# A selective-scan kernel: C rows held in SBUF between groups, their products written into b's buffers, the middle group's partitions in two halves

## The chip, the cores and the metric

One core of one Trainium2 chip runs the whole program. The metric is device time in microseconds of one execution, the median of three runs. All arithmetic that matters here is float32.

## The reference

Two "metaformer" layers on an image batch x of shape (2, 96, 128, 128). Layer 0 adds a four-direction Mamba block to the channel-normalised image, then a small quantised MLP; layer 1 adds a 3x3 convolution and another MLP. The Mamba block is what the change touches, and it takes most of the time. For each of four directions (rows, rows reversed, columns, columns reversed) and each position t of the 16,384 positions, with 192 inner channels d and 16 states s:

```
xc, z  = split(x @ in_w.T);  xc = silu(causal_conv4(xc) + conv_b)
dt_raw, B, C = split(xc @ xproj_w.T)          # 6, 16 and 16 numbers a position
dt = softplus(dt_raw @ dt_w.T + dt_b);  A = -exp(A_log)
h[d,s] = exp(dt[d] * A[d,s]) * h[d,s] + dt[d] * xc[d] * B[s]
y[d]   = sum_s h[d,s] * C[s] + Dp[d] * xc[d]
out    = (y * silu(z)) @ outp_w.T             # four directions joined by fuse_w
```

B and C depend on the position and the state, not on the channel. Each direction has its own.

## The kernel before

Each image of the batch goes through three stages: a normalisation, the Mamba stage (`mamba`), and the MLPs with the convolution (`ffn_and_conv`). Only the Mamba stage changes.

**Tiling.** Two directions are handled together (`PAIRS`): 2 x 192 = 384 channels are three groups (g = 0, 1, 2) of 128 partitions. Group 0 holds channels of the first direction, group 2 of the second, and group 1, the middle one, 64 of each. A step is 512 positions of one pair of directions: 32 steps for each of two pairs, so 64 for an image and 128 in all. Within a step and a group the 16 states are taken two at a time; such a pair of states is a unit, eight to a group (numbered 0 to 7 here) and 24 to a step. Four states, two units, are a quad.

**A unit's work.**

- ACT computes the decay exp(dt * A) into a PSUM tile `da`, two activations of 512 (`decay`, L349).
- DVE scans along the positions, once for each state (`scan`, L353). The result h replaces `da` in PSUM, or, for units in `BY_POOL`, the b tile in SBUF.
- h is multiplied by the C rows (128x1024): by DVE (L441) into the tile that holds the C rows, or by POOL in place for units in `BY_POOL` (L360), which here are units 0 and 4 of each group.
- PE adds the two halves of the product into one PSUM tile y by matmuls with the identity (`sums`, L357). An fp32 matmul shows as two PE instructions.
- Once in a quad, POOL multiplies the B rows (128x2048) by dt * xc in place (`b_part`, L339), two units ahead of the scan, and adds the entry state.

At a group's start DVE multiplies the finished y by silu(z) (`gated`, L364), and y's only buffer starts afresh with a matmul pair (L448). In the first and third group of a step PE also projects a finished group (`project`, L372 and L374).

**B and C rows.** They are computed as 64 rows of 512 numbers and stored in DRAM (`rows_to_dram`, L277). For each quad, two transfers bring the B rows (`row0`) and the C rows (`row1`) back, each spread over 128 partitions, 1 MB (`row_tile`, L335): 24 in a step. B has four buffers, fetched three quads ahead; C three, fetched two quads ahead. In the middle group the two directions lie on alternate partitions, so that one transfer serves both. To bring xc and silu(z) of the middle group into that order, ACT writes them to a tile `mix`, and two transfers of 64 partitions each put them on alternate partitions (`mix`, L256). The weights of the middle group are permuted to match (`_layout`, `perm`).

**Order.** It is written out by hand. Iteration k issues the first scan of unit k, then the product, the end-state copy (L442) and the sums of unit k-1 (`behind`), then the decay of unit k+2 and the second scan of unit k. Work of the next step (convolutions, gates, rows, dt) has fixed places in this order. `later(k, where, ...)` puts a job at iteration k, after its first part (0) or at its end (1): POOL's product of a `BY_POOL` unit at the end of the iteration after the unit, its sums two iterations later. All of the row transfers are issued by SP, in order; a transfer whose buffer is not yet free holds up those behind it. Which buffer a new tile takes is settled when the program is built: the one that comes free first in the written order.

Of the kernel before, what the change touches and what calls it, by code (L numbers as in the profile page):

```python
# [10 lines left out]
F32 = mybir.dt.float32  # L11
# [3 lines left out]
AF = mybir.ActivationFunctionType  # L15
ALU = mybir.AluOpType
# [13 lines left out]
HID = 384  # L30
PAIRS = ((0, 2), (1, 3))
NG = 3
B_AHEAD = 3
C_AHEAD = 2
AHEAD = 2
BY_POOL = tuple((g, s) for g in range(3) for s in (0, 8))
BCO = 32
NBC = 4 * S

# [2 lines left out]
def tile_metaformer(ctx: ExitStack, tc: tile.TileContext, a: dict, out: bass.AP):  # L42
# [142 lines left out]
    def mamba(acc, xnr, xnc):  # L185

        with ExitStack() as st:
            pool = lambda n, bufs, **kw: st.enter_context(tc.tile_pool(name=n, bufs=bufs, **kw))

            io, gen, one, mixp, two = (pool(*p) for p in (("io", 2), ("gen", 4), ("one", 1), ("mixp", 1), ("two", 2)))  # L190
            ps_w, ps_y, ps_m = (pool(n, k, space=PSUM) for n, k in (("ps_w", 3), ("ps_y", 1), ("ps_m", 1)))
            rows_d = pool("rows_d", 3, space=DRAM)

# [20 lines left out]
            def prologue(pi, i, d):  # L214
# [20 lines left out]
                def conv_out(g):  # L235
                    if g == 1:
                        d["xc"] = two.tile([128, NG, T], F32, name="xc")
                    t = mixed("xc") if g == 1 else d["xc"][:, g, :]
                    nc.scalar.activation(t, d["ps"], AF.Identity, bias=convb[:, pi, g : g + 1])  # L239

                def gate(g):
                    d["ps"] = inproj(pi, g, lambda dd, k, lo, hi: inz[:, dd, lo:hi], src, (3,))
# [1 line left out]
                def gate_out(g):  # L244
                    if g == 1:
                        d["sz"] = two.tile([128, NG, T], F32, name="sz")
                    nc.scalar.copy(mixed("sz") if g == 1 else d["sz"][:, g, :], d["ps"])  # L247

                def mixed(name):
                    d["mix", name] = mixp.tile([128, T], F32, name="mix")  # L250
                    return d["mix", name]

                def mix(name):

                    for k in range(2):
                        nc.sync.dma_start(d[name][k:128:2, 1, :], d["mix", name][64 * k : 64 * k + 64, :])  # L256

                def silu(name):
                    nc.scalar.activation(d[name], d[name], AF.Silu)
# [45 lines left out]


                first = pi == 0 and i == 0
                at = [(-3, 1, load), (3, 0, partial(mix, "xc")), (11, 0, partial(silu, "xc"))]
                at += [(9, 0, partial(mix, "sz")), (31, 1, partial(silu, "sz"))]
                at += [(12, 0, rows), (13, 1, rows_out), (14, 0, rows_to_dram)]  # L310
                for g, k in ((1, 1), (0, 5), (2, 9)):
                    at += [(k, 0, partial(conv, g)), (k + 1, 1, partial(conv_out, g))]
# [13 lines left out]
                at = [(k, where, getattr(f, "func", f) not in outs, f) for k, where, f in at]  # L326
                return sorted(at, key=lambda p: p[:3])

            def row_tile(d, g, s, k, ahead):

                t = gen.tile([128, 4, T], F32, name=f"row{k}", bufs=ahead + 1)

                src = d["bcd"][k, s // 4] if g == 1 else d["bcd"][k, s // 4, g // 2 : g // 2 + 1]
                n = src.shape[0]
                nc.sync.dma_start(t, src[None].broadcast_to((128 // n, n, 4, T)))  # L335
                return t

            def b_part(i, d, g, s, b):
                nc.gpsimd.tensor_tensor(b, d["dtu"][g][:, None, :].broadcast_to((128, 4, T)), b, ALU.mult)  # L339
# [17 lines left out]
                    nc.tensor.matmul(y, ident, c[:, j, :], start=False, stop=s + j == S - 1)  # L357

            def by_pool(h, c):
                nc.gpsimd.tensor_tensor(c, h, c, ALU.mult)  # L360

            def gated(pi, d, g, y):
                t = d["sz"][:, g, :]
# [26 lines left out]
            def later(k, where, rank, f, *args):  # L390
                todo.setdefault((k, where), []).append((rank, partial(f, *args)))
# [20 lines left out]
            prepare(1)  # L412
            bs, cs, das, hs, quads = {}, {}, {}, {}, {}

            def fetch(k, n, ahead, m):
                if k < total:
                    t = row_tile(state[k // nu], *units[k % nu], n, ahead)
                    m[k], m[k + 1] = t[:, 0:2, :], t[:, 2:4, :]
                    if n == 0:
                        quads[k] = t  # L420

            def feed(k):

# [11 lines left out]
            def behind(k):  # L435

                n, u = divmod(k, nu)
                (pi, i), d, (g, s) = steps[n], state[n], units[u]
                h, c = hs.pop(k), cs.pop(k)
                if (g, s) not in BY_POOL:  # L440
                    nc.vector.tensor_tensor(c, h, c, ALU.mult)  # L441
                nc.scalar.copy(hst[:, g, s : s + 2], h[:, :, T - 1])  # L442
                if s == 0:
                    if k > 0:
                        pn, pu = divmod(k - 1, nu)
                        gated(steps[pn][0], state[pn], units[pu][0], ys.pop(k - 1))
                    y = ps_y.tile([128, T], F32, name="y")
                    nc.tensor.matmul(y, dmat[:, pi, g, :], d["xc"][:, g, :], start=True, stop=False)  # L448
                else:
                    y = ys.pop(k - 1)  # L450
                ys[k] = y
                if (g, s) in BY_POOL:
                    later(k + 1, 1, True, by_pool, h, c)
                    later(k + 3, 1, True, sums, s, y, c)
                else:
                    sums(s, y, c)
                if k == total - 1:
                    gated(pi, d, g, y)
                if s == S - 2 and g > 0:
                    later(k + 4, 0, True, project, pi, i, d, g)  # L460
                    later(k + 5, 1, False, collect, pi, d, g)

            for m, (n, ahead) in ((bs, (0, B_AHEAD)), (cs, (1, C_AHEAD))):
                for k in range(ahead):
                    fetch(2 * k, n, ahead, m)
            feed(0)
            for k in range(AHEAD):
                feed_decay(k)
            for k in range(total + 6):
                n, u = divmod(k, nu)  # L470
                if u == nu - 3:

                    prepare(n + 2)
                if k % 2 == 0:
                    fetch(k + 2 * B_AHEAD, 0, B_AHEAD, bs)
                    feed(k + AHEAD)
                issue(k, 0)
                if k < total:
                    (g, s) = units[u]
                    da, b = das.pop(k), bs.pop(k)  # L480
                    hs[k] = b if (g, s) in BY_POOL else da
                    scan(0, da, b, hs[k])
                if 0 < k <= total:
                    behind(k - 1)
                feed_decay(k + AHEAD)
                if k < total:
                    scan(1, da, b, hs[k])
                if k % 2 == 0:
                    fetch(k + 2 * C_AHEAD, 1, C_AHEAD, cs)
                issue(k, 1)  # L490

    def ffn_and_conv(b, acc):
# [107 lines left out]
def _layout(v):  # L600

    f = np.float32
    order = [d for pair in PAIRS for d in pair]

    perm = np.arange(2 * DI)
    perm[128:256] = perm[128:256].reshape(2, 64).T.reshape(-1)
    grouped = lambda w: w.reshape(2, NG, 128, -1).transpose(2, 0, 1, 3)
    plain = lambda w: grouped(w[order].reshape(2, 2 * DI, -1))
    rows = lambda w: grouped(w[order].reshape(2, 2 * DI, -1)[:, perm])
    xw = v["L0_conv_xproj_w"]  # L610
    bcw = np.zeros((2, 2 * DI, BCO + NBC), f)
    dtw = np.zeros((2 * RK, 2, 2 * DI), f)
    for pi, pair in enumerate(PAIRS):
        for k, d in enumerate(pair):
            at = slice(k * DI, (k + 1) * DI)
            for j in range(2):

                to = [BCO + 2 * j * S + 8 * (s // 4) + 4 * k + s % 4 for s in range(S)]
                bcw[pi, at, to] = xw[d, RK + j * S : RK + (j + 1) * S]
            bcw[pi, at, k * RK : (k + 1) * RK] = xw[d, :RK].T  # L620
            dtw[k * RK : (k + 1) * RK, pi, at] = v["L0_conv_dt_w"][d].T
    outx = np.zeros((C, 2, NG + 1, 128), f)
    for pi, (p, q) in enumerate(PAIRS):
        ow = v["L0_conv_outp_w"]
        outx[:, pi, 0] = ow[p, :, :128]
        outx[:, pi, 1, 0::2] = ow[p, :, 128:]
        outx[:, pi, 2, 1::2] = ow[q, :, :64]
        outx[:, pi, 3] = ow[q, :, 64:]
    out = {
        "x": v["x"].reshape(NB, C, L),  # L630
        "ident": np.eye(128, dtype=f),
        "inx": v["L0_conv_in_w"][:, :DI].transpose(2, 0, 1),
        "inz": v["L0_conv_in_w"][:, DI:].transpose(2, 0, 1),
        "taps": v["L0_conv_conv_w"].transpose(0, 2, 1)[None],
        "convb": plain(v["L0_conv_conv_b"])[..., 0],
        "bcw": grouped(bcw[:, perm]),
        "dtw": dtw[:, :, perm],
        "dtb": rows(v["L0_conv_dt_b"])[..., 0],
        "alog": rows(v["L0_conv_A_log"]),
        "dskip": rows(v["L0_conv_Dp"])[..., 0],  # L640
        "outx": outx,
        "fusew": v["L0_conv_fuse_w"].reshape(C, 4, C).transpose(2, 1, 0),
        "fuseb": v["L0_conv_fuse_b"].reshape(C, 1),
        "kw": v["L1_conv_kernel"].transpose(1, 2, 3, 0).reshape(C, 9, C),
    }
    for n in range(2):
        p = f"L{n}_ffn_"
        out[f"w1_{n}"] = v[p + "W1"].T
        out[f"b1_{n}"] = v[p + "b1"].reshape(3, 128).T
        out[f"w2_{n}"] = v[p + "W2"].T.reshape(3, 128, C).transpose(1, 0, 2)  # L650
        out[f"b2_{n}"] = v[p + "b2"].reshape(C, 1)
    return {k: np.ascontiguousarray(w) for k, w in out.items()}
# [16 lines left out]
```

## Time and profile before

| | us |
|---|---|
| median of 3 runs | 11546.39 (11545.31 to 11548.33) |
| the profiled execution, its own time | 11556.77 |
| its span | 11555.0 |
| DVE busy | 10421.6 |
| PE busy | 10435.0 |
| POOL busy | 9672.3 |
| ACT busy | 7901.7 |
| POOL b products (L339), 1536 | 6948.9, mean 4.524 |
| DVE scans (L353), 4608 into da and 1536 into row | 5456.9 and 1852.4, means 1.214 and 1.206 |
| DVE C products (L441), 2304 | 2776.7, mean 1.205 |
| POOL C products (L360), 768 | 1807.4, mean 2.353 |
| DVE gated products (L364) | 264.6, mean 0.689, idle ahead of them 229.5 |
| row transfers, 3072 of 1 MB | median 7.4 from issue to landing |

3416.96 MB were moved by DMA. A group's line on the page gives its busy time, its mean in ns, and the idle time of the engine just before its instructions with what ended it. A wait line gives the waiting engine and line, what it waited for, the total in us, the times and the longest. A timeline line gives start, duration, engine, line, operation and tiles; "x3" stands for three merged in a row. DVE instructions overlap slightly: one starts about 1.12 us after the one before, though each record is 1.2 long.

### The profile page before, as it was taken

How to read it: one execution, taken by the hardware profiler on the slowest of the kernel's cores; microseconds unless marked ns; L12 is line 12 of the kernel's file. 1: busy time of each engine (PE TensorE's matmuls, PEld its weight loads, DVE VectorE, ACT ScalarE, POOL GpSimd, SP SyncE). 2: the span in 40 equal slices, each digit the busy share in tenths (PEclk: the TensorE clock that was granted, in tenths of full speed). 3: DMA queues.
4: the chain of work that ended last, by engine and by line, in shares of the span. 5: the costliest groups of instructions: out<-in, count | busy, mean ns of one | idle time of the engine just before them, and what ended most of it. 6: DMA issues, size and time to landing. Idle time of an engine off the chain costs nothing. (4 is left out here: it accounts for less than half of the span.)

```text
span 11555.0 us, 94102 instructions
## 1 busy us (share of the span) xinstructions
PE 10435.0 (90%) x24208; PEld 3971.4 (34%) x24208; DVE 10421.6 (90%) x10127; ACT 7901.7 (68%) x13564; POOL 9672.3 (84%) x4700
## 2 busy tenths in 40 slices
PE   7999999999999999989989999999999999999899
PEld 2333333333333333333323333333333333333333
DVE  6999999999999999994469999999999999999944
ACT  6767767677677677665567677677676776776655
POOL 5999999999999999991159999999999999999911
PEclk8999999999999999999989999999999999999999
DMA  7888888888888888880068888888888888888800
GB/s 263 335 329 333 333 332 332 330 331 333 329 332 333 330 331 333 329 322 19 26 243 334 328 331 334 330 333 333 333 331 329 332 332 329 331 333 329 319 13 13
DMA packets 540755, 3416.96 MB, mean 296 GB/s; under 512 B 67532, under 2 KB 68652, under 8 KB 143832
## 3 DMA queue, kind: packets, MB, share of 16 engines
q1 hardware_dynamic: 539960, 3410.16, 76.8%
q8 instruction: 196, 3.21, 0.1%
q14 instruction: 343, 2.81, 0.1%
q0 software_dynamic: 256, 0.79, 0.0%
HBM read 3289.04 MB, written 54.53 MB: 289 GB/s over the span
## 5 line engine op out<-in xcount | busy, mean ns | idle before, releaser
L339 POOL TENSOR_TENSOR row<-dtu,row 128x2048 f32<-128x2048 f32 x1536 | 6948.9, 4524 | 283.3 <-DMA row<-bcd 281.6
L357 PE MATMUL y<-row,ident 128*128 128x512 f32 x12288 | 5690.6, 603 | 700.0 <-DVE row L441 699.9
L353 DVE TENSOR_TENSOR_SCAN da<-da,row 128x512 f32<-128x512 f32 x4608 | 5456.9, 1214 | 38.9 <-ACT da L349 5.2
L349 ACT ACTIVATE da<-dt,amat 128x512 f32<-128x512 f32 x6144 | 4246.9, 691 | 170.2
L357 PEld LDWEIGHTS y<-row,ident 128*128 128x128 f32 x12288 | 2256.8, 190 | 4008.4 <-issue 2243.5
L441 DVE TENSOR_TENSOR row<-da,row 128x1024 f32<-128x1024 f32 x2304 | 2776.7, 1205 | 70.2 <-DMA row<-bcd 70.0
L442 ACT COPY hst<-da 128x2 f32<-128x2 f32 x2304 | 368.9, 160 | 2652.2 <-DVE row L441 2649.3
L360 POOL TENSOR_TENSOR row<-row,row 128x1024 f32<-128x1024 f32 x768 | 1807.4, 2353 | 223.0 <-DVE row L353 147.5
L353 DVE TENSOR_TENSOR_SCAN row<-da,row 128x512 f32<-128x512 f32 x1536 | 1852.4, 1206 | 91.9 <-POOL row L339 84.1
L211 PE MATMUL misc<-xa,inx 96*64 96x512 f32 (+1 forms) x2048 | 946.1, 605 | 50.0 <-ACT mix L239 26.8
L211 PE MATMUL misc<-xb,inx 96*64 96x512 f32 (+1 forms) x2048 | 952.3, 608 | 33.6 <-ACT hst L442 24.2
L564 POOL TENSOR_TENSOR acc<-acc,y 96x512 f32<-96x512 f32 x128 | 147.4, 1151 | 991.5 <-DVE y L563 991.5
L298 POOL TENSOR_TENSOR dtu<-dt,xc 128x512 f32<-128x512 f32 x384 | 487.4, 1269 | 106.0 <-DMA xb<-xnc 99.8
L576 PE MATMUL pc<-pad,kw 96*96 96x512 f32 x1152 | 566.4, 593 | 0.0
L211 PEld LDWEIGHTS misc<-xa,inx 96*64 96x64 f32 (+1 forms) x2048 | 327.3, 165 | 581.2 <-issue 438.0
L448 PE MATMUL y<-xc,dmat 128*128 128x512 f32 x768 | 419.5, 628 | 103.6 <-DVE sz L364 103.6
L374 PE MATMUL misc<-sz,gmat 128*96 128x512 f32 x1024 | 484.1, 595 | 0.0
L284 PE MATMUL misc<-rows,dtw 12*128 12x512 f32 x768 | 434.3, 645 | 50.6 <-ACT dt L289 37.9
L364 DVE TENSOR_TENSOR sz<-y,sz 128x512 f32<-128x512 f32 x384 | 264.6, 689 | 229.5 <-PE y L357 198.0
L136 DVE TENSOR_TENSOR xq<-xm,rs 96x512 fp8e5<-96x512 f32 x128 | 87.9, 687 | 392.2 <-ACT rs L132 392.2
L211 PEld LDWEIGHTS misc<-xb,inx 96*64 96x64 f32 (+1 forms) x2048 | 316.5, 164 | 361.9 <-issue 214.1
L372 PE MATMUL misc<-acc,ident 96*96 96x512 f32 x512 | 387.6, 842 | 57.3 <-ACT sz L247 53.8
(76 smaller groups left out, 7449.9 us busy)
## 6 DMA issues: line engine op xcount, KB each, us to landing
row<-bcd SPq DMA_DIRECT2D x3072, 1024.0 KB, 7.4
xc<-mix SPq DMA_DIRECT2D x256, 128.0 KB, 5.4
sz<-mix SPq DMA_DIRECT2D x256, 128.0 KB, 8.9
xa<-xnr SPq DMA_DIRECT2D x124, 193.1 KB, 8.6
xb<-xnc SPq DMA_DIRECT2D x124, 193.1 KB, 8.7
bcd<-rows SPq DMA_DIRECT2D x128, 128.0 KB, 9.5
acc<-in_x_dram SPq DMA_DIRECT2D x16, 768.0 KB, 5.7
xnr<-xn SPq DMA_DIRECT2D x16, 768.0 KB, 4.3
```

Source lines behind the costliest of these rows:

```text
L211: nc.tensor.matmul(ps[rows, :], w(PAIRS[pi][d], k, lo, hi), src[d][:, k : k + T], **se)
L284: nc.tensor.matmul(d["ps"], w, d["rows"][0 : 2 * RK, :], start=True, stop=True)
L298: nc.gpsimd.tensor_tensor(dtu, d["dt"][:, g, :], d["xc"][:, g, :], ALU.mult)
L339: nc.gpsimd.tensor_tensor(b, d["dtu"][g][:, None, :].broadcast_to((128, 4, T)), b, ALU.mult)
L349: nc.scalar.activation(da[:, j, :], d["dt"][:, g, :], AF.Exp, scale=amat[:, pi, g, s + j : s + j + 1])
L353: nc.vector.tensor_tensor_scan(h[:, j, :], da[:, j, :], b[:, j, :], 0.0, ALU.mult, ALU.add)
L357: nc.tensor.matmul(y, ident, c[:, j, :], start=False, stop=s + j == S - 1)
L360: nc.gpsimd.tensor_tensor(c, h, c, ALU.mult)
L374: nc.tensor.matmul(d["po"], gmat[:, pi, 2 * g - 2 + k, :], d["yg"][g - 1 + k], start=False, stop=k == 1)
L441: nc.vector.tensor_tensor(c, h, c, ALU.mult)
L448: nc.tensor.matmul(y, dmat[:, pi, g, :], d["xc"][:, g, :], start=True, stop=False)
L576: nc.tensor.matmul(pc, kw[:, t, :], rows, start=t == 0, stop=t == 8)
```

## The change

C rows no longer pass through rotating buffers. Four tiles `crow0` to `crow3` (128x2048, one for each quad of states) stay in SBUF. Before each new group only the partitions whose direction differs are refilled (`c_fill`): all 128 for group 0, the upper 64 for group 1, the lower 64 for group 2. In the middle group the first direction now lies on partitions 0-63 and the second on 64-127, so the `mix` tile and its transfers go, the weights are no longer permuted, and a B quad of the middle group comes as two transfers of 64 partitions.

A C quad can't be overwritten by its product any more, so the product goes into the unit's half of the b tile, which then stays in use until PE has added it up. B has five buffers (fetched four quads ahead, at the end of an iteration). POOL's units are 1 and 4 of each group. The scratch memory [...] is set to 4096.

```diff
-B_AHEAD = 3
-C_AHEAD = 2
+B_AHEAD = 4
-BY_POOL = tuple((g, s) for g in range(3) for s in (0, 8))
+BY_POOL = tuple((g, s) for g in range(3) for s in (2, 8))
@@ conv_out, gate_out
-                    t = mixed("xc") if g == 1 else d["xc"][:, g, :]
-                    nc.scalar.activation(t, d["ps"], AF.Identity, bias=convb[:, pi, g : g + 1])
+                    nc.scalar.activation(d["xc"][:, g, :], d["ps"], AF.Identity, bias=convb[:, pi, g : g + 1])
-                    nc.scalar.copy(mixed("sz") if g == 1 else d["sz"][:, g, :], d["ps"])
-                def mix(name):
-                    for k in range(2):
-                        nc.sync.dma_start(d[name][k:128:2, 1, :], d["mix", name][64 * k : 64 * k + 64, :])
+                    nc.scalar.copy(d["sz"][:, g, :], d["ps"])
@@ row tiles
-            def row_tile(d, g, s, k, ahead):
-                t = gen.tile([128, 4, T], F32, name=f"row{k}", bufs=ahead + 1)
-                src = d["bcd"][k, s // 4] if g == 1 else d["bcd"][k, s // 4, g // 2 : g // 2 + 1]
-                n = src.shape[0]
-                nc.sync.dma_start(t, src[None].broadcast_to((128 // n, n, 4, T)))
+            def row_tile(d, g, s):
+                t = gen.tile([128, 4, T], F32, name="row", bufs=B_AHEAD + 1)
+                for part, k in (((slice(0, 64), 0), (slice(64, 128), 1)) if g == 1 else ((slice(0, 128), g // 2),)):
+                    src = d["bcd"][0, s // 4, k]
+                    nc.sync.dma_start(t[part], src[None].broadcast_to((part.stop - part.start, 4, T)))
                 return t
+            crow = [one.tile([128, 4, T], F32, name=f"crow{q}") for q in range(S // 4)]
+            def c_fill(n, g, q):
+                if n < len(steps):
+                    part = (slice(0, 128), slice(64, 128), slice(0, 64))[g]
+                    src = state[n]["bcd"][1, q, int(g > 0)]
+                    nc.sync.dma_start(crow[q][part], src[None].broadcast_to((part.stop - part.start, 4, T)))
...
             def by_pool(h, c):
-                nc.gpsimd.tensor_tensor(c, h, c, ALU.mult)
+                nc.gpsimd.tensor_tensor(h, h, c, ALU.mult)
@@ behind
-                h, c = hs.pop(k), cs.pop(k)
+                h, b, c = hs.pop(k), cs.pop(k), crow[s // 4][:, s % 4 : s % 4 + 2, :]
                 if (g, s) not in BY_POOL:
-                    nc.vector.tensor_tensor(c, h, c, ALU.mult)
+                    nc.vector.tensor_tensor(b, h, c, ALU.mult)
...
-                    later(k + 1, 1, True, by_pool, h, c)
-                    later(k + 3, 1, True, sums, s, y, c)
+                    later(k + 1, 1, True, by_pool, b, c)
+                    later(k + 3, 1, True, sums, s, y, b)
                 else:
-                    sums(s, y, c)
+                    sums(s, y, b)
@@ main loop
-            for m, (n, ahead) in ((bs, (0, B_AHEAD)), (cs, (1, C_AHEAD))):
-                for k in range(ahead):
-                    fetch(2 * k, n, ahead, m)
+            for k in range(B_AHEAD):
+                fetch(2 * k)
+                c_fill(0, 0, k)
...
                 if k % 2 == 0:
-                    fetch(k + 2 * B_AHEAD, 0, B_AHEAD, bs)
                     feed(k + AHEAD)
...
                     scan(1, da, b, hs[k])
                 if k % 2 == 0:
-                    fetch(k + 2 * C_AHEAD, 1, C_AHEAD, cs)
+                    fetch(k + 2 * B_AHEAD)
+                    if 4 <= k < total + 4:
+                        cn, cu = divmod(k - 4, nu)
+                        cg, cq = cu // 8, cu % 8 // 2
+                        c_fill(cn + (cg == 2), (cg + 1) % 3, cq)
                 issue(k, 1)
@@ _layout: perm is gone
-        outx[:, pi, 1, 0::2] = ow[p, :, 128:]
-        outx[:, pi, 2, 1::2] = ow[q, :, :64]
+        outx[:, pi, 1, :64] = ow[p, :, 128:]
+        outx[:, pi, 2, 64:] = ow[q, :, :64]
@@ kernel
-    nc = bacc.Bacc("TRN2", target_bir_lowering=False, num_devices=1)
+    nc = bacc.Bacc("TRN2", target_bir_lowering=False, num_devices=1, dynamic_dma_scratch_size=4096)
```

In the changed file the scan is at L350, the products at L436 (DVE) and L357 (POOL), the b product at L336, the gated product at L361, the sums at L354, the fetches of B at L323 and the refills of C at L333.

## The prediction

> **What bounds the kernel now.** I read the page first (busy time, slices, costliest groups), then one step of the scan stage, the waits of a steady stretch, SP's own waits, and the DVE, PE and SP timelines of one group.
>
> ```profile
> PE 10435.0 (90%) x24208; PEld 3971.4 (34%) x24208; DVE 10421.6 (90%) x10127; ACT 7901.7 (68%) x13564; POOL 9672.3 (84%) x4700
> ```
>
> One step (78.9 us: 76 gated products, L364, in 2000 us give 25.3 steps), by windows; columns are us, then busy us of PE, PEld, DVE, ACT, POOL:
>
> ```profile
> 2040.00:2118.90 78.90, 71.84 (x167) 27.12 (x166) 76.33 (x69) 55.74 (x97) 74.31 (x37) 1.00 0.87 333
> ```
>
> DVE is the bound: 76.3 of 78.9 us. The 128 steps make 10,099 of 11,555 us. Waits from 2000 to 4000 us (us, times, longest):
>
> ```profile
> DVE sz L364 <- PE y L357: 38.8, 41, 1.1
> DVE row L441 <- DMA row<-bcd: 12.7, 25, 0.9
> ```
>
> All DVE idle time there is 66 us, 2.6 a step: 1.8 ahead of L364, 0.5 at L441 for C rows, 0.3 elsewhere. That is all a change that leaves DVE's instructions alone can win: 2.6 x 128 = 330 us.
>
> SP waits too, in order, with everything queued behind:
>
> ```profile
> SPq L335 <- PE y L357: 1366.3, 279, 9.5
> ```
>
> The C fetches already wait for the sums that free their buffer. Middle of a group of the first kind, DVE, then PE, then SP:
>
> ```profile
> 2050.51 1.20 DVE L441 TENSOR_TENSOR row<-da,row 128x1024 f32<-128x1024 f32 x1
> 2051.63 1.21 DVE L353 TENSOR_TENSOR_SCAN row<-da,row 128x512 f32<-128x512 f32 x1
> 2052.76 3.58 DVE L353 TENSOR_TENSOR_SCAN da<-da,row 128x512 f32<-128x512 f32 x3
> 2056.25 1.21 DVE L441 TENSOR_TENSOR row<-da,row 128x1024 f32<-128x1024 f32 x1
> 2057.38 2.33 DVE L353 TENSOR_TENSOR_SCAN da<-da,row 128x512 f32<-128x512 f32 x2
> 2060.21 1.22 DVE L441 TENSOR_TENSOR row<-da,row 128x1024 f32<-128x1024 f32 x1 [0.50 <-DMA row<-bcd]
> ```
> ```profile
> 2049.05 1.90 PE L374 MATMUL misc<-sz,gmat 128*96 128x512 f32 x4
> 2050.78 5.31 PE L357 MATMUL y<-row,ident 128*128 128x512 f32 x12
> ```
> ```profile
> 2054.41 0.32 SPq L335 DMA_DIRECT2D row<-bcd  x1
> ```
>
> The product of unit 3 (2050.51) and that of unit 6 (2060.21, 0.50 of it waiting) lie 9.1 to 9.2 us apart without the wait. PE's 12 matmuls are the sums of units 2, 0 and 3, 1.72 us each; the C fetch of unit 6 leaves at 2054.41, when unit 0's sums end, and lands 5.8 us later, 0.5 late. This chain, sums to SP to transfer to product, is the one to watch.
>
> ```profile
> row<-bcd SPq DMA_DIRECT2D x3072, 1024.0 KB, 7.4
> acc<-in_x_dram SPq DMA_DIRECT2D x16, 768.0 KB, 5.7
> ```
>
> Transfers: with nothing ahead a 1 MB row load lands 5.1 us after its issue (4.71, 5.01, 5.12, 5.21, 5.52 between 2065 and 2119 us); queued ones land 2.5 us apart (2097.17, 2099.67, 2102.16, 2104.64). The 768 KB loads into 96 partitions at the start land 3.0 us apart (18.89, 21.90, 24.93, 27.89): fewer partitions are not faster.
>
> [...]
>
> **The change, part by part.** Durations are of the profiled execution (span 11555.0, its own time 11556.77; the median of the runs is 11546.39, 0.1% less).
>
> *Work.* DVE, POOL, PE and ACT keep their counts and shapes. L441's output goes to the b buffer, POOL's product stays in place: 0.
>
> *Traffic.* Rows were 24 MB a step; now 12 B MB and 8 C MB. The number doesn't fall: 24 + 4 mix transfers become 12 of 1 MB and 16 of 512 KB into 64 partitions. No row shows a half. Its ends: 1.25 us (by bytes), and 3.0 (what a 96-partition load takes in all, if its first 64 partitions are what holds it up). I take 2.5, an estimate: [...]. Then 28 x 2.5 = 70 us of transfer a step against 24 x 2.5 = 60, in spite of fewer bytes.
>
> *Gains.* Unit 0's product is now DVE's and stands ahead of L364, which so comes 1.12 us later; the longest L364 wait in the stretch is 1.1, so 1.8 us go. The 0.5 for C goes or is renamed. Total 2.6 at most, which leaves 76.3 a step. If PE were later still, L364 would keep some of its 1.8.
>
> *mix, weights, scratch size.* Four 128 KB transfers a step go, hidden now (no DVE wait names them). Weight order is free. [...] Fills before the first unit grow from 5 to 8 MB: 2 x 7.5 us at most, 0 taken; the b part comes first.
>
> *The new wait.* A b buffer was free after POOL's or DVE's use; now after PE's sums. The built program says whose: the fetch of iteration 2 in each group takes the buffer of units 2-3, so SP stands until unit 3's sums, two iterations later; behind it in the queue is the refill of C quad 3 for the *same* group (in the first group the full quad, behind two b halves), which unit 6's product needs. A group without stalls is 22 DVE instructions 1.12 apart and L364's 0.6, 25.25 us; twelve of them and L364 stand ahead of unit 3's product, which starts at 14.05. From there:
> - Sums of unit 3 end after 1.2 (product) + 2.0 (four matmuls, 1.98 when alone) = 3.2 when PE is free (third group); 3.65 in the first, where conv and projection are ahead (conv ends 7.9 after the group's start; then y's first matmul pair 0.9, sums of unit 0 1.75, projection 3.6, units 2 and 3 3.5: 17.7; the product starts at 14.05); 4.15 in the second, where the rows matmuls (2.74) are ahead.
> - SP 0.2, first landing 5.1, each further one 2.5. First group: 3.65 + 0.2 + 5.1 + 2.5 + 2.5 = 13.95; second: 4.15 + 0.2 + 5.1 + 2.5 = 11.95; third: 3.2 + 0.2 + 5.1 + 2.5 = 11.0.
> - Allowed: 9.1. Late by 4.85, 2.85, 1.9: 9.6 us. Behind the waiting product stand unit 7's second scan on DVE, the sums of units 6, 4 and 7 on PE, the end-state copies and decays of ACT; they are late with it, and nothing overtakes on DVE.
> - What is late next: after the first group's quad 3 (28.0 from its start) three more halves end at 35.5, with C quad 0 of the second group last; unit 8's product wants it at 25.25 + 4.85 + 4.5 = 34.6: 0.9. The next three are issued after unit 4's sums (33.1), end at 43.2; unit 10 wants quad 1 at 41.7: 1.5. Full and half alternate later and catch up.
>
> POOL's b tiles still come in time: the first group's fetch for units 10-11 lands at 25.5, POOL needs 4.7 for it, the scan wants it at 25.25 + 4.85 + 7.3 = 37.4; POOL (74.3 us) and PE (71.8) have room in a longer step.
>
> Sum: 76.3 + 9.6 + 2.4 = 88.3 a step, +9.4; x 128 = +1200: profile 12,755, median about 12,750.
>
> **Rivals.**
> 1. Halves cost by bytes, 1.25. Late: first group 3.65 + 0.2 + 3.85 + 1.25 + 2.5 - 9.1 = 2.35; second 4.15 + 0.2 + 5.1 + 1.25 - 9.1 = 1.6; third 0.65; no knock-on. 76.3 + 4.6 = 80.9, +2.0 x 128: 11,800. For: fewer bytes. [...] If a low and a high half overlap [...], the first two groups are each 2.85 late and the third 1.9: 83.9, near 12,190.
> 2. Halves at 3.0. First group 4.85 + 1.0, others + 0.5 each, knock-ons 2.3 and 2.8: some 17 us late, +14.4 x 128: 13,400.
> 3. The other side: quad 3 arrives in time, only the gains remain, 11,546 - 330 = 11,220. It needs the transfers within 9.1 - 3.4 = 5.7 us of SP's release, two or three at once, where one alone takes 4.7 to 5.5. It decides below that. For: 1.25 us halves and an idle queue come near it. Against: even with PE free, the quickest landing (4.71) and halves by bytes, the third group needs 3.2 + 0.2 + 4.7 + 1.25 = 9.35 of its 9.1. A partial miss that just eats the 2.6 is "the same".
>
> **How the numbers follow.** Main case 0.62 (own range 12,450 to 13,050), rival 1 with its overlap form 0.24, rival 2 0.07, rival 3 0.04, a draw 0.03. A measurement of this kernel can tell about 0.2%. Slower 0.93, same 0.03, faster 0.04. Leaving out rival 3, the draw and most of rival 2 gives 11,750 to 13,200.
>
> **What would show it.** The product (now L436) waiting for a DMA into the C quads 10 to 13 us a step, some 1500 us in all, mostly at unit 6, longest in first groups; L361 (gated) idle under 60 us in place of 229; scan, products and POOL means unchanged; about 2.81 GB moved in place of 3.42, with a DMA share that hardly falls; POOL and PE idle more. Wrong if halves land 1.3 us apart, if SP is released earlier than unit 3's sums, or if POOL's b tiles come late and the scan waits instead.

## The result and the profile after

The changed kernel takes 13,685.49 us (median of 4 runs, 13,671.92 to 13,694.54) against 11,546.12 us: a ratio of 1.185, 95% interval 1.183 to 1.187. It is slower, as forecast, but by 2,139 us where 1,200 were forecast, and 485 us above the top of the range.

The page of the kernel after: busy time and number of instructions of each engine, then the TensorE clock and the DMA engines' busy share over 40 equal slices, then what was moved.

```profile
PE 11228.8 (82%) x24208; PEld 4289.7 (31%) x24208; DVE 10511.3 (77%) x10127; ACT 7948.0 (58%) x13564; POOL 9683.2 (71%) x4700
...
PEclk8999999989999989999989999999999999999999
DMA  7777777777777777772067777777777777777720
...
DMA packets 442445, 2812.93 MB, mean 206 GB/s; under 512 B 67532, under 2 KB 68652, under 8 KB 111064
```

DVE's busy time grew by 90 us (10,421.6 before) and POOL's by 11, with the same instructions: no engine got more work. PE shows 794 us more for the same 24,208 instructions, so its matmuls got longer. 2.81 GB were moved, as forecast, and the transfers still keep the DMA engines busy for 70% of a longer span (77% before).

The costliest groups of the page (out<-in, count, busy us, mean ns, then the idle time just ahead of them and what ended most of it):

```profile
L354 PE MATMUL y<-row,ident 128*128 128x512 f32 x12288 | 6485.0, 673 | 1905.1 <-DVE row L436 1068.2
L336 POOL TENSOR_TENSOR row<-dtu,row 128x2048 f32<-128x2048 f32 x1536 | 6937.3, 4517 | 584.4 <-DMA row<-bcd 550.0
L350 DVE TENSOR_TENSOR_SCAN da<-da,row 128x512 f32<-128x512 f32 x4608 | 5456.4, 1214 | 92.8 <-POOL row L336 53.0
...
L436 DVE TENSOR_TENSOR row<-da,crow 128x1024 f32<-128x1024 f32 x2304 | 2788.3, 1210 | 1983.7 <-DMA crow<-bcd 1982.2
...
L357 POOL TENSOR_TENSOR row<-row,crow 128x1024 f32<-128x1024 f32 x768 | 1808.4, 2355 | 2062.1 <-ACT hst L437 1992.9
...
L361 DVE TENSOR_TENSOR sz<-y,sz 128x512 f32<-128x512 f32 x384 | 264.9, 690 | 383.2 <-PE y L354 371.7
```

The same three rows of the kernel before (sums, DVE's product, POOL's product):

```profile
L357 PE MATMUL y<-row,ident 128*128 128x512 f32 x12288 | 5690.6, 603 | 700.0 <-DVE row L441 699.9
...
L441 DVE TENSOR_TENSOR row<-da,row 128x1024 f32<-128x1024 f32 x2304 | 2776.7, 1205 | 70.2 <-DMA row<-bcd 70.0
...
L360 POOL TENSOR_TENSOR row<-row,row 128x1024 f32<-128x1024 f32 x768 | 1807.4, 2353 | 223.0 <-DVE row L353 147.5
```

Nearly all of the loss stands in one row: L436, the product with C, waits 1,983.7 us for transfers into the C quads (70.2 before), 15.5 us in each of the 128 steps. L361, the gated product, waits 383.2 us, 3.0 a step, where the forecast had none left. The scans wait 0.7 a step. Means of scans, products and POOL's b products are those of before; the sums on PE (L354) went from 603 to 673 ns.

One such wait, from where it starts. The chain of waits of the kernel after, from 2,055 to 2,095 us (start, us, what; each piece is what released the next):

```profile
2057.40 3.45 PE y L354 x8
...
2060.91 0.45 SPq L323
...
2061.40 0.60 SPq L323
...
2062.04 8.50 DMA crow<-bcd
...
2070.63 1.24 DVE row L436
...
2072.00 6.65 PE y L354 x8
...
2078.70 0.44 SPq L323
...
2081.11 12.21 DMA crow<-bcd
```

PE's sums free a b buffer; only then SP issues the two b halves that waited for it (L323), and behind them the C refill, which lands 8.50 us after its issue, 9.63 after SP was released; the product of unit 6 (2,070.63) waited for it; and the next release hangs on the sums behind that product. This is the chain that the forecast described. What it did not have is the length of the last PE piece: 6.65 us for eight PE instructions, the sums of two units, where the same eight took 3.45 at the top. The windows over the stall (us, busy us of PE, PEld, DVE, ACT, POOL, then PE's clock, DMA share and GB/s):

```profile
2060.00:2066.00 6.00, 6.00 (x15) 2.64 (x15) 5.91 (x6) 3.59 (x8) 5.31 (x2) 1.00 0.69 162
2066.00:2072.00 6.00, 2.72 (x8) 0.62 (x8) 1.37 (x2) 0.80 (x2) 5.81 (x4) 0.93 1.00 292
2072.00:2077.00 5.00, 5.00 (x6) 2.14 (x7) 5.00 (x5) 4.89 (x6) 2.11 (x3) 0.50 0.94 192
```

While DVE stands still PE has nothing to do, and in the next 5 us its granted clock is 0.50.

### The profile page after: what moved, and what is told of

Same layout as the page of the kernel before. It is cut to its first block, busy times and chain, and to the rows that moved or that the text cites. A ratio compares the mean times of both kernels' runs of the same rounds, so it can differ in the third digit from the quotient of the medians.

```text
span 13674.8 us, 93092 instructions
## 1 busy us (share of the span) xinstructions
PE 11228.8 (82%) x24208; PEld 4289.7 (31%) x24208; DVE 10511.3 (77%) x10127; ACT 7948.0 (58%) x13564; POOL 9683.2 (71%) x4700
## 4 chain that ended last, share of the span: by engine, by line
PE 45%; DMA 24%; POOL 11%; issue 10%; DVE 5%; ACT 3%; SPq 2%; POOLq 0%; DVEq 0%; ACTq 0%
PE y L354 25%; DMA crow<-bcd 20%; POOL row L336 8%; PE misc L210 5%; DMA row<-bcd 4%; PE pc L575 4%; DVE row L436 3%; PE misc L255 2%; POOL row L357 2%; PE misc L371 2%; SPq L323 2%; PE misc L369 2%; PE xm L121 2%; PE v L127 2%; PE y L443 1%
## 5 line engine op out<-in xcount | busy, mean ns | idle before, releaser
L354 PE MATMUL y<-row,ident 128*128 128x512 f32 x12288 | 6485.0, 673 | 1905.1 <-DVE row L436 1068.2
L336 POOL TENSOR_TENSOR row<-dtu,row 128x2048 f32<-128x2048 f32 x1536 | 6937.3, 4517 | 584.4 <-DMA row<-bcd 550.0
L350 DVE TENSOR_TENSOR_SCAN da<-da,row 128x512 f32<-128x512 f32 x4608 | 5456.4, 1214 | 92.8 <-POOL row L336 53.0
L436 DVE TENSOR_TENSOR row<-da,crow 128x1024 f32<-128x1024 f32 x2304 | 2788.3, 1210 | 1983.7 <-DMA crow<-bcd 1982.2
L354 PEld LDWEIGHTS y<-row,ident 128*128 128x128 f32 x12288 | 2538.3, 213 | 5633.6 <-issue 5138.5
L357 POOL TENSOR_TENSOR row<-row,crow 128x1024 f32<-128x1024 f32 x768 | 1808.4, 2355 | 2062.1 <-ACT hst L437 1992.9
L350 DVE TENSOR_TENSOR_SCAN row<-da,row 128x512 f32<-128x512 f32 x1536 | 1851.3, 1205 | 0.0
L361 DVE TENSOR_TENSOR sz<-y,sz 128x512 f32<-128x512 f32 x384 | 264.9, 690 | 383.2 <-PE y L354 371.7
L371 PE MATMUL misc<-sz,gmat 128*96 128x512 f32 x1024 | 517.8, 630 | 0.0
L255 PE MATMUL misc<-xc,bcw 128*96 128x512 f32 x768 | 407.7, 672 | 7.1 <-ACT xc L248 7.1
## 6 DMA issues: line engine op xcount, KB each, us to landing
crow<-bcd SPq DMA_DIRECT2D x512, 1024.0 KB, 10.1
```

The costliest lines, as they stand in the source:

```text
L255: nc.tensor.matmul(d["ps"][0 : BCO + NBC, :], bcw[:, pi, g, :], d["xc"][:, g, :], start=g == 0, stop=g == NG - 1)
L350: nc.vector.tensor_tensor_scan(h[:, j, :], da[:, j, :], b[:, j, :], 0.0, ALU.mult, ALU.add)
L357: nc.gpsimd.tensor_tensor(h, h, c, ALU.mult)
L371: nc.tensor.matmul(d["po"], gmat[:, pi, 2 * g - 2 + k, :], d["yg"][g - 1 + k], start=False, stop=k == 1)
L436: nc.vector.tensor_tensor(b, h, c, ALU.mult)
```

## The experiments

Three theories. **A, the queue**: SP stands on PE's sums for a b buffer with the C refill behind it. **B, the halves**: 28 transfers a step of about 2.5 us each are more than the queue delivers in time, whatever their order. **C, the clock**: the halved TensorE clock after each stall doubles the sums that release the next buffer, and makes what the forecast missed. "A step" is the mean over the 128 steps of the trace, and a wait is the idle time just ahead of an instruction. The wait ahead of the first scan of each of the two images is in these means (0.4 us a step in the kernel after, 0.6 in the kernel before).

**C refills ahead of the fetch.**

```diff
-                    fetch(k + 2 * B_AHEAD)
                     if 4 <= k < total + 4:
                         ...
                         c_fill(cn + (cg == 2), (cg + 1) % 3, cq)
+                    fetch(k + 2 * B_AHEAD)
```

> Two lines change places: in each iteration the C refill is issued ahead of the b fetch, so no C quad stands on SP behind the wait for a b buffer. Theory A (the order of the queue: SP stands on PE's sums with the C refill behind it): the product's waits on the C quads, 15.4 us a step at units 2, 6, 8, 10, 14 and 22, nearly all go, TensorE no longer idles and its half-clock windows go, a step takes 76.5 to 79 us: 11,250 to 11,700. Theory B (28 transfers a step, the halves as dear as full ones, are more than the queues carry in time whatever the order): the waits only move to other units or to the scans, a step stays at 88 us or more: above 12,700.

12,050.64 us, ratio 1.043 (1.041 to 1.045). Two lines exchanged give back 1,635 of the 2,139 us. The page's groups, of this kernel:

```profile
L336 POOL TENSOR_TENSOR row<-dtu,row 128x2048 f32<-128x2048 f32 x1536 | 6950.7, 4525 | 917.4 <-DMA row<-bcd 869.6
L350 DVE TENSOR_TENSOR_SCAN da<-da,row 128x512 f32<-128x512 f32 x4608 | 5519.7, 1217 | 514.2 <-POOL row L340 412.4
L436 DVE TENSOR_TENSOR row<-da,crow 128x1024 f32<-128x1024 f32 x2304 | 2779.3, 1206 | 212.6 <-DMA crow<-bcd 209.8
```

The product's wait fell from 1,983.7 to 212.6 us. But theory A wanted 11,250 to 11,700; now the b rows come late: POOL waits 870 us for them, and the scans 412 for POOL. So the time lies between the two ranges: A is the larger part, and not the whole.

**Fetch three quads ahead, with the same five buffers.**

```diff
-B_AHEAD = 4
+B_AHEAD = 3
-                t = gen.tile([128, 4, T], F32, name="row", bufs=B_AHEAD + 1)
+                t = gen.tile([128, 4, T], F32, name="row", bufs=B_AHEAD + 2)
```

(with all four C quads still filled at the start)

> Five b buffers as before, but the fetch runs three quads ahead instead of four, so each fetch takes a buffer that has been free for a quad longer and SP should stand on PE's sums less; the C refill of quad 3 then comes ahead of the fetch that waited on unit 3's sums. Theory A: as with the C refills first, 11,300 to 11,800. Theory B: above 12,700. If the smaller lead leaves POOL's b tiles late instead, the scan waits for POOL and the time is 12,000 to 12,700.

12,060.13 us, 1.044 (1.042 to 1.047): another way of getting the refill of quad 3 ahead of the wait, and the same time within 10 us, with the same remainder (6.4 us of waits a step, 6.7 above). It bears out A's part a second time. But the time lies in the third range, not in A's: here too POOL waits 864 us for b rows.

**Halves over every other partition.**

```diff
-for part, k in (((slice(0, 64), 0), (slice(64, 128), 1)) if g == 1 else ...
+for part, k in (((slice(0, 128, 2), 0), (slice(1, 128, 2), 1)) if g == 1 else ...
-                    part = (slice(0, 128), slice(64, 128), slice(0, 64))[g]
+                    part = (slice(0, 128), slice(1, 128, 2), slice(0, 128, 2))[g]
```

> The halves of the middle group's b rows and of the C refills go to every other partition instead of to partitions 0 to 63 or 64 to 127; number, size and order of the transfers are unchanged. (Its middle group then has its rows on other partitions than the weights: the results of that group are not the reference's.) If a half costs 2.5 us [...], it now costs about 1.25; the stalls of units 6, 14 and 22 fall from 4.4, 3.7 and 3.1 us to about 2.3, 1.6 and 0.6 and those of units 2 and 10 nearly vanish: 8 to 11 us a step less, 12,250 to 12,650. If the price of a half is per transfer, nothing changes: 13,600 to 13,750.

12,444.14 us, 1.077 (1.075 to 1.080): 1,241 us less, with every byte and every instruction the same. Halves of one stretch land at 2,056.07, 2,057.31 and 2,058.53 us, 1.2 apart, where those of the kernel after land 2.5 apart (2,065.44, then 2,067.93). Over the whole trace a half that was issued behind another transfer lands 1.25 us after it (median of 1,344), in the kernel after 2.43 (of 1,349). The DMA rows of its page:

```profile
DMA  6666666666666666661056666666666666666600
...
DMA packets 442445, 2812.93 MB, mean 227 GB/s; under 512 B 67532, under 2 KB 68652, under 8 KB 111064
```

Share 0.6 in place of 0.7, at more bytes per second. So a half into 64 neighbouring partitions does cost nearly what a whole one does (2.43 us, a whole quad 2.7), because of where it goes. A and B are both at work; each edit alone gives more than half of the loss back, so the two gains overlap.

**Both together.** The two edits above in one kernel.

> Both edits together: C refills ahead of the fetch, halves on every other partition. (The middle group's results are not the reference's.) If halves cost 1.25 us [...], a step moves 12 halves of b and C less: 16 x 1.25 + 12 x 2.5 = 50 us of transfers in place of 70, and what the C refills first leave (6.7 us of waits a step) goes nearly all: 11,150 to 11,450, below the kernel before. If halves cost the same there, 12,000 to 12,100.

11,646.69 us, 1.008 (1.007 to 1.010). The page's groups:

```profile
L350 DVE TENSOR_TENSOR_SCAN da<-da,row 128x512 f32<-128x512 f32 x4608 | 5498.7, 1216 | 402.9 <-POOL row L340 273.1
L436 DVE TENSOR_TENSOR row<-da,crow 128x1024 f32<-128x1024 f32 x2304 | 2774.2, 1204 | 0.1
L357 POOL TENSOR_TENSOR row<-row,crow 128x1024 f32<-128x1024 f32 x768 | 1809.5, 2356 | 571.4 <-ACT hst L437 570.9
```

The waits for C are gone to the last tenth of a microsecond, and with them 95% of the loss; yet it is 100 us slower than before, not 100 to 400 faster. What is left are scans that wait (3.1 us a step), mostly for POOL, and POOL's product L357, which waits 571 us for ScalarE's end-state copy.

**The middle group's b quad in one transfer, C refills first.**

```diff
+                    src = d["bcd"][0, s // 4]
+                    nc.sync.dma_start(t, src[:, None].broadcast_to((2, 64, 4, T)))
```

> C refills first as before, and the middle group's b quad comes in one transfer into all 128 partitions (its source read as two halves of 64 copies) in place of two: 24 transfers of about 2.5 us a step instead of 28, 60 us instead of 70. With the C refills first alone a step waits 6.7 us, 3.7 of it scans waiting for POOL, whose b rows land late. If that is the backlog of transfers in the middle group, a step waits 1 to 3 us: 11,250 to 11,600. If it is POOL waiting for ScalarE's end-state copies, no change from 12,050 by more than 100.

20,853.7 us, 1.806 (1.803 to 1.809): neither. Windows of 10 us while such a transfer runs:

```profile
2137.00:2147.00 10.00, 4.96 (x6) 2.19 (x7) 5.99 (x6) 4.96 (x6) 4.88 (x3) 0.50 0.18 59
2147.00:2157.00 10.00, 6.63 (x15) 2.61 (x13) 0.96 (x1) 2.67 (x5) 0.00 (x0) 0.97 0.13 52
```

A DMA share of 0.13 is what two of 16 engines make when they are always busy, and 52 GB/s are 1 MB in 20 us. The outermost dimension of this transfer has size 2; the kernel before, whose middle quads have the 64 copies outermost, lands them 2.5 us behind the transfer ahead (median of 765). Why the order of the dimensions costs this much was not shown. This run says nothing on A or B.

**POOL on units 0 and 4 again.**

```diff
-BY_POOL = tuple((g, s) for g in range(3) for s in (2, 8))
+BY_POOL = tuple((g, s) for g in range(3) for s in (0, 8))
```

> POOL again multiplies units 0 and 4 of each group, as in the kernel before, instead of 1 and 4. The third iteration's fetch still waits for the sums of its quad. Theory A: no stall is removed, since the sums of units 2 and 3 still free the buffer; quad 3 may be 1 to 2 us earlier, the gated product loses the cover of unit 0's product and waits up to 1.8 us more a step: 12,900 to 13,700. Theory B: no change, 13,600 to 13,750.

13,066.55 us, 1.131 (1.130 to 1.133): 619 us better. The wait of unit 6 stays (4.48 us a step, 4.44 with the changed kernel), those of units 14 and 22 fall from 3.68 and 3.06 to 1.19 and 1.74, and the gated product's rise from 2.99 to 4.53. The time lies in theory A's wide range, though that expected no stall to go. So the choice of POOL's units, which the forecast counted as a gain, cost 4.7 us a step here. The traces show how. With POOL on units 0 and 4, unit 0's sums stand ahead of unit 3's in the written order, so the fetch of the third iteration takes the buffer of units 0 and 1, and in all three groups SP is released by unit 0's sums, where the kernel after waits for unit 3's. In the second group PE takes up unit 3's sums only behind the matmuls of the rows: SP issues 23.6 us after the group's first scan in the kernel after, 21.1 here (means), and these 2.5 us are what unit 14's wait falls by. In the third group the sums come earlier as a block. In one step of each kernel, with unit 0's sums ahead of the gate's matmuls, ScalarE's copy of the gate and the projection behind it start 1.6 us later (16.12 us after unit 14's product, 14.52 here), and with them the sums that release SP (22.44 and 20.84). So the premise of this forecast, that the sums of units 2 and 3 still free that buffer, did not hold.

**Does that hold once the queue is in order?** The same edit on the kernel with the C refills first.

> The changed kernel with the C refills first, and POOL on units 0 and 4. With the refills second, that choice of units was worth 620 us. If it was worth that because of POOL's wait for ScalarE and what that delays, it is worth several hundred here too: 11,500 to 11,800. If it was worth that only through the queue behind the sums of POOL's units, which the order of the queue has dealt with, 12,000 to 12,150.

11,895.67 us, 1.029 (1.027 to 1.032), 155 us below the C-first kernel and between the two ranges. With the queue in order the choice of units costs 155 us of the 619; the other three quarters needed the refill's place behind SP's wait.

**Keeping TensorE busy behind the stall.** Three matmuls with a weight of zeros, added into y, ahead of the sums of unit 6, and of unit 2 in the first two groups.

```diff
+                    if s == 12 or (s == 4 and g < 2):
+                        for _ in range(3):
+                            nc.tensor.matmul(y, zero_w, d["dt"][:, g, :], start=False, stop=False)
                     sums(s, y, b)
```

> Three matmuls with a weight of zeros (2.6 us of TensorE at full clock) are put ahead of the sums of unit 6 in each group and of unit 2 in the first two groups, where TensorE idles behind a waiting product; the sum they are added to is unchanged. Theory C (TensorE's clock halves in the windows in which it idles, which doubles the block of sums after the stall, makes the gated product wait and the next buffers late): the granted clock rises from 0.92 to above 0.96, the gated waits fall from 3.0 to under 1 us a step, the product's waits at units 2, 10 and 14 get shorter, 4 to 5 us a step fewer: 13,000 to 13,250. If the clock is only a symptom: no gain, or up to 2 us a step more (13,650 to 13,950).

13,686.12 us, 1.185 (1.183 to 1.187): no change, although the mean clock rose from 0.916 to 0.960. The gated waits fell from 2.99 to 0.5 us a step, and unit 6's rose from 4.44 to 6.38: zeros ahead of unit 2's sums delay the very sums that release SP. In the second group they gain: the sums of unit 10, at a mean clock of 0.70 in the kernel after, have the full clock and take 1.9 us in place of 2.9; SP issues 4.3 us after unit 11's product starts in place of 5.5, and unit 14 waits 2.65 us a step, not 3.68. Next only unit 6's were kept:

```diff
-                    if s == 12 or (s == 4 and g < 2):
+                    if s == 12:
```

> The three zero matmuls stand ahead of the sums of unit 6 alone, where TensorE waits for the stalled product anyway; those ahead of unit 2's sums, which delayed the sums that free the buffer of the third fetch (the stall of unit 6 grew from 4.4 to 6.4 us with them), are left out. Theory C (the halved clock after the stall costs time): clock above 0.95, the gated product's waits fall from 3.0 to about 0.5 us a step and units 10 and 14 by 1 each, unit 6 stays at 4.4: 13,050 to 13,350. If the halved clock is only a symptom: 13,600 to 13,800.

13,686.87 us, 1.185 (1.183 to 1.187), again no change. Gated waits 0.6, unit 10 down by 1.04 us a step, but unit 22 up by 1.96 and its scan by 0.95. The PE timeline of this kernel (its lines stand two further down than those of the kernel after), at the start of the third group, tells where the gain went:

```profile
2195.05 1.03 PE L212 MATMUL misc<-xa,inz 96*128 96x512 f32 x2
2199.45 2.02 PE L371 MATMUL misc<-acc,ident 96*96 96x512 f32 x2 [3.38 <-ACT hst L439]
2201.27 3.62 PE L373 MATMUL misc<-sz,gmat 128*96 128x512 f32 x4
```

DVE comes earlier into the third group, but ScalarE, behind its softplus, is no earlier, so PE idles there, for 3.38 us, and its clock halves at this place instead: the four matmuls of L373 take 3.62 us (1.88 for the same four in the kernel after). One more kernel puts two zero matmuls there too:

```diff
+                    if s == 12 or (g, s) == (2, 0):
+                        for _ in range(3 if s == 12 else 2):
```

> Zero matmuls at unit 6 as in the run before, and two more at the start of the third group, where TensorE otherwise idles 3.4 us behind ScalarE and its clock halved there instead. If the halved clock costs time and had only moved, the stall of unit 22 falls back from 5.0 to about 3 us: 13,250 to 13,450. If it is a symptom (the third group's first sums are late for ScalarE's softplus, whatever the clock), 13,600 to 13,750.

13,423.97 us, 1.161 (1.160 to 1.163); unit 22 back at 3.28. Holding the clock up gained 262 us, 2.0 us a step, by matmuls that compute nothing. It is a cost, then, and by these runs the smallest of the three. It is a lower bound: the mean clock is 0.967 here, not the 0.989 of the kernel before, and 0.76 at the sums of unit 10, ahead of which no zeros stand in this run.

**One part alone in the kernel before.** POOL on units 1 and 4, all else as before.

```diff
-BY_POOL = tuple((g, s) for g in range(3) for s in (0, 8))
+BY_POOL = tuple((g, s) for g in range(3) for s in (2, 8))
```

> The kernel before with one part of the change alone: POOL multiplies units 1 and 4 of each group in place of 0 and 4, into the C tile as before. The prediction's gain: unit 0's product stands ahead of the gated product, whose waits (1.75 us a step) go: 11,310 to 11,400. If instead the C rows of unit 0 or POOL's later products make new waits of the same size: 11,500 to 11,650.

12,106.02 us, 1.048 (1.046 to 1.049), above both ranges. The groups:

```profile
L353 DVE TENSOR_TENSOR_SCAN da<-da,row 128x512 f32<-128x512 f32 x4608 | 5487.0, 1215 | 472.3 <-POOL row L343 340.7
L441 DVE TENSOR_TENSOR row<-da,row 128x1024 f32<-128x1024 f32 x2304 | 2778.8, 1206 | 421.6 <-DMA row<-bcd 417.7
```

The gated wait does what was forecast (34 us in all, 229.5 before), and gets eaten nearly four times over: the C rows of unit 22 come 3.0 us late a step, b rows make POOL late (L339 waits 853 us for them, 282 before), and POOL the scans. Moving POOL's product one unit later holds its C tile for longer, and SP's fetches stand behind that tile; SP's own waits from 2,000 to 4,000 us:

```profile
SPq L335 <- POOL row L360: 341.1, 95, 7.8
```

In the kernel before this wait is 19.1 us.

**Looking for a version that beats both.** The interleaved channels of the kernel before (with its four small transfers and its order of weights), so that C halves go to every other partition and a middle b quad comes in one transfer as there, with the C refills first. The tile `dtu` has three buffers here and in the next run, where the other kernels have four:

```diff
+                    t = mixed("xc") if g == 1 else d["xc"][:, g, :]
...
+                src = d["bcd"][0, s // 4] if g == 1 else d["bcd"][0, s // 4, g // 2 : g // 2 + 1]
+                n = src.shape[0]
+                nc.sync.dma_start(t, src[None].broadcast_to((128 // n, n, 4, T)))
...
+                    part = (slice(0, 128), slice(1, 128, 2), slice(0, 128, 2))[g]
```

> The changed kernel with three things altered: C refills ahead of the fetch; the middle group's channels interleaved again (and its weights with them, with the four small transfers that interleave its convolution's and gate's results), so that its b rows come in one transfer and a C half goes to every other partition. By the timing of the two edits on their own (C first, alternate partitions), 16 x 2.5 + 8 x 1.25 = 50 us of transfers a step and waits of 2.5 to 4 us: 11,450 to 11,700. If only POOL's wait for ScalarE's end-state copy is left, the scans of units 0, 8 and 22 wait 0.5 to 1.1 us each, as with those two edits.

11,860.73 us, 1.027 (1.026 to 1.028), above the range. No product waits for C (0.1 us in all), but the first scan of unit 13 waits 1.44 us a step for ScalarE and the gated product of the second group 1.47: neither was foreseen. The profile names no wait for a `dtu` buffer (POOL's L297 waits 94 us in all, for ScalarE and for inputs; 106 in the kernel before), but four buffers were not run. With POOL on units 0 and 4:

> The interleaved kernel with the C refills first, and POOL on units 0 and 4 as in the kernel before. Unit 4's end-state copy then stands ahead of softplus on ScalarE, so POOL's in-place product should not wait for it: if that wait is what keeps the interleaved kernel at 11,861, this takes 11,500 to 11,650 (the gated waits of the kernel before, 1.75 us a step, come back). If it stays above 11,750, the reason is another.

11,972.02 us, 1.037 (1.035 to 1.038), worse. POOL's wait for the end-state copy did not go (938 us in all, 803 with units 1 and 4), so the reason given for this run falls, and why the interleaved kernel stays 300 us above the kernel before remains open. No version here beats 11,546 us.

## Why the prediction was right or wrong

The waits on DVE, us a step: as forecast, in the kernel after, and with the clock held up by zero matmuls.

| wait ahead of | forecast | after | clock held |
|---|---|---|---|
| product of unit 2 | 0 | 1.14 | 1.21 |
| product of unit 6 | 4.85 | 4.44 | 4.65 |
| product of unit 8 | 0.9 | 0.52 | 0.45 |
| product of unit 10 | 1.5 | 2.65 | 1.62 |
| product of unit 14 | 2.85 | 3.68 | 3.70 |
| product of unit 22 | 1.9 | 3.06 | 3.28 |
| gated products | 0 | 2.99 | 0.51 |
| scans and others (0.39 of both measured ones at the images' starts) | 0 | 0.74 | 1.78 |
| sum | 12.0 | 19.2 | 17.2 |

The forecast's step was 76.3 + 12.0 = 88.3 us; the measured one is 96.1, of which 18.8 are waits inside the step and 77.3 the rest. The rest grew because fewer of DVE's records overlap: its busy time rose by 90 us, 0.7 a step.

**Right.** The new wait and its chain: the buffer freed by PE's sums, SP standing, the C quad behind it, the product late, worst in the first group. The trace shows each link, and putting the C refills first took 1,635 us away. The half at 2.5 us, an estimate for which the trace of the kernel before held no half: 2.4 us between landings in the median, and 1.25 when the same half goes to every other partition. Rival 1 (halves by bytes, 11,800) is what that run would be: it took 12,444, because even at 1.25 us the refills stand behind SP's wait. Rival 2 (halves at 3.0 us) has the number nearest to the measured one, 13,400, but not its cause. 2.81 GB were right; an idle L436 of "10 to 13 us a step" was too low (15.5).

**Wrong, the gains' step** ("1.8 us go", 2.6 in all). L361 waits more than before, not less. It holds without stalls: in the kernel before with POOL's units moved the gated wait does vanish. But that same edit lost 553 us there, with C tiles held for longer and b rows late, and putting POOL's units back gains 619 in the changed kernel. The step looked only at the wait that goes. It left out the buffer that POOL's later product keeps for longer, the projection that comes later, and that the choice of units decides whose sums release SP. "POOL's product stays in place: 0" belongs here too: POOL now overwrites h, so it waits for ScalarE's copy of it (1,993 us of POOL's idle time after). Most of that only follows DVE's stalls; with those gone 571 us of it are left, beside scans that wait for POOL. That this wait causes them was not separated.

**Wrong, a cost left at nothing: PE at full clock.** The step took a unit's sums at 1.72 to 2.0 us throughout, and said of PE and ACT that "they are late with it". In the kernel after the sums of units 6, 14 and 22 take 3.5, 3.1 and 3.3 us (1.9 to 2.0 before), at a mean clock of 0.56, 0.63 and 0.59. PE idles while it is late, and the idling halves its clock: at least 2.0 us a step by the zero matmuls, and with it go nearly all of unit 10's excess and of the gated waits. In the trace of the kernel after the clock records are 1.0 or 0.5, their lengths are multiples of 3.41 us, and 386 of PE's 425 idle times of 3 us and more are followed by one of 0.5. So are 131 of the 231 between 2 and 3 us, and 12 of the 406 from 0.2 to 2 us. The forecast put PE's work behind a wait of 4.85 us and priced nothing for it.

**Wrong in size, SP's release in the second and third group.** In the three groups SP issues the fetch 3.8, 5.5 and 4.7 us after unit 3's product starts (means of the some 107 steps whose landings the trace tells), where the forecast's terms give 3.85, 4.35 and 3.4; C quad 3 lands 9.8, 7.2 and 7.5 us later (forecast 10.1, 7.6 and 7.6). So the first group's sum was right, and the other two are late by the release, not by the transfers. "Sums of unit 3 end after 3.2 when PE is free (third group)": PE is not free there, since the projection waits for ScalarE behind softplus. That is the 1.1 us by which unit 22 is off. In the second group the sums of unit 10, ahead of those that release SP, run at a halved clock after unit 10's own stall. The last column does not hold it up there (2.7 us for these sums); the first run with zeros does, and there unit 14 waits 2.65 us. So unit 14's extra 0.8 is the clock's too. Unit 2's wait (1.1) was not foreseen, and its cause is open.

In all, 6.8 us of waits in a step were missed. Of these the last run with zeros shows 2.0 to be the clock's, and unit 14's 0.8 comes to that. The choice of POOL's units makes 4.7 us a step by its run, though part of that lies inside the waits that the forecast did have; so the exact split is open. The `mix` transfers that go and the scratch size were not run alone.

## What to carry to other kernels

When a buffer's release moves to a later engine, list what stands behind the wait in the same queue, and put what does not need that buffer ahead of it: two lines exchanged were worth 1,635 us here. Price a transfer by the partitions it reaches, not by its bytes alone: here 512 KB into 64 neighbouring partitions landed 2.43 us behind the transfer ahead, into every other one 1.25. When an operation moves to a later place, ask which buffer the next fetch takes and whose work now frees it. And when a forecast makes the matrix engine wait for more than 2 to 3 us, price its next matmuls at half the clock (here a record of 0.50 followed 386 of 425 idle times of 3 us and more, and 131 of 231 between 2 and 3), then look at whether the time won at one stall only comes back at the next.

## What the runs showed of the hardware

- 512 KB into 64 neighbouring partitions land 2.4 us apart in the median, like 1 MB into 128 (2.7 in the same trace); into every other partition 1.25 us apart. With that edit alone the 8 KB packets between 2,000 and 4,000 us go from 624 ns (75th percentile) to 309, near the 316 of the kernel before.
- TensorE's clock falls to 0.50 after the stall of one late transfer, though PE was 82% busy on the whole; idle times of 2 to 3 us were enough in 131 of 231 cases. Multiplications by zero for 2.8 us hold it up (mean 0.947 to 0.967 with them, 0.916 without), but in three kernels with them the time changed by 0, 0 and -262 us: what they gain at one stall can come back at the next.
- A broadcast whose outermost dimension is 2 moved 1 MB in 20 us at 52 GB/s, with a DMA share of 0.13; in the kernel before the same bytes with the 64 copies outermost land 2.5 us behind the transfer ahead.
